# A two-layer graph kernel: three dense row chunks in place of four, and the staging order around them

## The chip, the cores and the metric

The kernel runs on one core of a Trainium2 chip. The metric is the device time of one execution in microseconds; lower is better.

## The reference

`x` is 8 x 2048 x 128 (batch, nodes, features), `adj` is a 2048 x 2048 matrix with few entries that are not zero (some nine a row). Cut to what matters:

```python
# layer 0
sj, si = inputs @ w_j, inputs @ w_i
res = si[:, :, None] + sj[:, None, :] + relation[None] * w_r + g_b
agg = einsum('bij,bjd->bid', res, inputs)
x = layernorm(x + agg @ weight + bias)
# layer 1: hops 1 and 2 over the same matrix, twice the same set of hops
x1 = einsum('bnf,nw->bwf', x0, A)
x2 = 2.0 * einsum('bnf,nw->bwf', x1, A) - x0
x = layernorm(x + relu(concat([x0, x1, x2, x1, x2]) @ Theta1 + bias))
```

So layer 0 multiplies by the rows of the matrix, layer 1 twice by its columns. All sums are in float32.

## The kernel before, in words

The nodes are cut into 16 chunks of 128. All eight batches of a chunk stand side by side: a tile of 128 x 1024 numbers, 512 KB.

**Three passes.** Layer 0 makes `y = x @ weight` for all chunks first, so that one pass over the matrix gives `agg @ weight`. Layer 1 becomes two hops with the weights folded in (`thetas`): hop 1 reads `u`, which `make_u` (lines 650 to 659) makes from the output of layer 0, and writes `y_d`; hop 2 reads `y_d` and writes the output. `make_u` transposes eight blocks of a chunk on PE, multiplies them by theta and stores 512 KB of u.

**Dense and listed chunks.** In layer 0 the first `ND` = 4 chunks of rows are multiplied in full: `full_rows` (lines 311 to 318) does 16 x 2 matmuls of 128x512 for a chunk (two records each in the profile), with the transposed rows of the matrix held in `at4`. The other twelve chunks, and all chunks of the two hops, are "listed": the matrix rows that matter for 32, 64 or 128 columns of the chunk are gathered by number. The lists are made on the chip: `mask_rows` and `mask_columns` mark the blocks that hold anything, VectorE ranks them, and `lists_end` writes row numbers into `idx`. A chunk has seven lists: four "T" lists for 32 columns each (rows of the first 14 chunks), two "H" lists for 64 columns and one for 128. For each list GpSimd (POOL) issues one indirect gather of 128 rows of 4 KB out of y, u or y_d (`get_rows`, lines 724 to 730), and `listed` (lines 732 to 755) multiplies them by the "set", the matching 128 x 384 numbers of the matrix. The diagonal block of a listed chunk is done apart: `load_own` (lines 765 to 773) has SP load the chunk's own rows and the 128 x 128 block `rd`, and `own_rows` does two matmuls.

**Sets.** A listed chunk needs two sets, one of the transposed rows for layer 0 (in `rct`) and one of the columns for the hops (in `rc`). Their sources are put side by side in DRAM: `store_rt` stores the transposed rows of a chunk into `rr_d` (1 MB), `copies` copies the matrix columns beside it (1 MB, DRAM to DRAM). `get_job` (lines 532 to 540) gathers out of `rr_d` into one of four staging buffers in `st`, with four gathers for a chunk's T lists or three for its H lists; `keep_job` (lines 542 to 563) takes them out on VectorE with four operations, two of them for each set. There are 24 such jobs, first the T jobs of all listed chunks, then the H jobs; `next_job` is a keep and a get. A get can start when the keep four jobs earlier is through. Chunks 0 to 3 have no layer-0 set, and the hop's set comes directly out of `adj`, in seven gathers a chunk (`get_direct`, lines 578 to 583), 28 in all, after `clear` has zeroed its place.

**Order.** Each engine's order is written out by hand and kept, save that the scheduler may put POOL's row gathers of the next chunk ahead of a staging gather. POOL carries the staging gathers, row gathers and directs in one queue. Row gathers go round twelve slots in `Y` (list `G`), so a gather waits until PE is through with the one twelve earlier. VectorE does, for a listed chunk of layer 0, `keep_job`, `z_add` and `layernorm` in this order. SP's queue loads the matrix, x, z (the residual x of a chunk), own rows and diagonals. The start goes: transposes and masks while the matrix arrives (to about 105 us), y and the lists, dense chunks 0 to 3 with staging beside them (lines 787 to 849), then the loop over the listed chunks:

```python
    for c in range(ND, NC):
        ...
        if kept[0] < len(jobs):
            keep_job()
        if got[0] < len(jobs):
            get_job()
        get_direct((c > 7) + (c > 9))
        accs = acc_pair()
        own_rows(0, c, accs, True)
```

Hop 1 starts with the T gathers of three chunks, for which u of chunks 0 to 13 must be stored; `make_u(15)` stands on PE behind the first chunk's T matmuls, and the H gathers wait for it.

Of the kernel before, what the change touches and what calls it, by code (L numbers as in the profile page):

```python
# [8 lines left out]
F32 = mybir.dt.float32  # L9
# [9 lines left out]
def kernel(  # L19
# [22 lines left out]
    P = 128  # L42
# [4 lines left out]
    TW = 32  # L47
    NT = N // TW
    QT = P // TW
    ND = 4  # L50
    NS = NC - ND
    LT = 14
    LR = LT // 2
    HC = NT // 2 + NC
    NI = NT + HC
    PAD = 40000
    W = 3 * P
    T_ORDER = list(range(6, NC)) + [4, 5]
    NP = LR + NC - LT
    R_ORDER = [0, 1, 4, 5, 6, 2, 7, 8, 9, 10, 3, 11, 12, 13, 14, 15]  # L60
    NX = 8
    X_ORDER = list(range(ND, NC)) + list(range(ND))
    X_SLOT = [0, 1, 3, 4, 2, 5]
    assert D == P and B == 8 and NC == 16

# [21 lines left out]

    Y = keep.tile([P, NC, B, D], F32, name="Y")
    rc = keep.tile([P, NC * W], F32, name="rc")
    rct = keep.tile([P, NS * W], F32, name="rct")  # L90
# [8 lines left out]
    def flat(t):  # L99
        return t.rearrange("p b f -> p (b f)")  # L100
# [79 lines left out]

    am = [rc[:, n * N:(n + 1) * N] for n in range(3)]
    ats = [rct[:, n * N:(n + 1) * N] for n in range(2)]
    ats += [Y[:, n:n + 2].rearrange("p c b f -> p (c b f)") for n in X_ORDER[NX::2]]

    def at_of(c):
        t = at4[:, c] if c < ND else ats[(c - ND) % len(ats)]
        return t.rearrange("p (j i) -> p j i", i=P)

    def x_at(k):
# [11 lines left out]
    todo += [("x", 8), ("s", 12), ("x", 9), ("s", 13), ("x", 10), ("x", 11), ("s", 14), ("x", 12)]  # L201
    todo += [("s", 15), ("x", 13), ("x", 14), ("x", 15)] + [("c", c) for c in T_ORDER]
    done = {"a": 0, "x": 0}

    def load_x(c, t):
# [10 lines left out]
    def pump():  # L216
        while todo:
            what, n = todo[0]
            if what == "a" and n < done["a"] + 3:
                sp.dma_start(out=am[n % 3], in_=adj[R_ORDER[n] * P:(R_ORDER[n] + 1) * P, :])  # L220
            elif what == "x" and n < done["x"] + 6:
                c = X_ORDER[n]
                xin[c] = load_x(c, ring[:, X_SLOT[n % 6]])
                if c < ND:
                    zs[c] = xin[c]
            elif what == "s" and done["a"] == NC:
                store_rt(n)
            elif what == "c" and done["a"] == NC:
                copies([n])
            else:  # L230
                return
            todo.pop(0)
# [72 lines left out]
                    tile_position=(0, 32 * j),  # L305
                )

    LAST = list(range(ND)) + list(range(8, NC)) + list(range(4, 8))
    js_first = [X_ORDER[0]] * 2 + [LAST[0]] * (ND - 2)

    def full_rows(c, accs, js):
# [211 lines left out]
    def strided(t, n, step, w):  # L523
        return t[:, 0:n * step].rearrange("p (n s) -> p n s", s=step)[:, :, 0:w]

    jobs = [("T", c) for c in T_ORDER] + [("H", c) for c in range(ND, NC)]
    got, kept = [0], [0]

    def staged(k):
# [12 lines left out]
    def keep_job():  # L542
        what, c = jobs[kept[0]]
        s = staged(kept[0])
        kept[0] += 1
        hc = has[:, columns(c, what)[0]:columns(c, what)[0] + QT]
        for k in range(2):
            to = rc[:, c * W:(c + 1) * W] if k else rct[:, (c - ND) * W:(c - ND + 1) * W]
# [168 lines left out]
    load_z(4)  # L717

    NG = 12
    G = [flat(Y[:, n]) for n in LAST[:NG]]  # L720
    g_at = [0]
    rows_of = {}

    def get_rows(i, c, what, src):
        hi = LT if what == "T" else NC
        for n, q in enumerate(columns(c, what)):
            g = G[g_at[0] % NG]
            g_at[0] += 1
            gather(g, src[0:hi * P, :], idx, q, hi * P)
            rows_of[i, c, what, n] = g  # L730

    def listed(i, c, accs, what):

        r = rc[:, c * W:(c + 1) * W] if i else rct[:, (c - ND) * W:(c - ND + 1) * W]
# [26 lines left out]
    homes = [seven[(c + 8) % 12 % 7] for c in range(12)] + [slab(k) for k in range(4)]  # L761
    u_of = [ring[:, 2]] * 12 + homes[12:]
    own = {}

    def load_own(i, src, c, t, there=False):
        if not there:
            sp.dma_start(out=flat(t), in_=src[c * P:(c + 1) * P, :])
        r = small.tile([P, P], F32, name=f"rd{i}_{c}", tag="rd", bufs=2)
        sp.dma_start(
            out=r, in_=rr_d[c - ND][c * P:(c + 1) * P, 0, :] if i == 0  # L770
            else adj[c * P:(c + 1) * P, c * P:(c + 1) * P],
        )
        own[i, c] = t, r

    def own_rows(i, c, accs, start):
        t, r = own.pop((i, c))
# [15 lines left out]
    for c0 in range(0, NC, 4):  # L792
        column_sums(c0)
    make_ub()
    load_z(ND + 1)
    rounds2([4])
    next_job()
    si_t(0)
# [12 lines left out]
    layernorm(zs[0], "0_0")  # L811

    acc2 = bank[4:6]
    full_rows(2, acc2, LAST[:5])
    next_job()
    next_job()
    make_u(0, zs[0], x1t[0], u_of[0], 0)
    layernorm(zs[1], "0_1")
    full_rows(2, acc2, LAST[5:11])
    next_job()  # L820
    make_u(1, zs[1], x1t[1], u_of[1], 0)
    next_job()
    next_job()
    next_job()
    full_rows(2, acc2, LAST[11:])
    si_t(2)
    rank9(2, acc2)
    z_add(acc2, zs[2])
    overflow()
    next_job()  # L830
    layernorm(zs[2], "0_2")

    acc3 = bank[2:4]
    full_rows(3, acc3, LAST[:8])
    next_job()
    next_job()
    get_rows(0, ND, "T", y0_d)
    get_rows(0, ND, "H", y0_d)
    own0(ND)
    own0(ND + 1)  # L840
    full_rows(3, acc3, LAST[8:])
    keep_job()
    keep_job()
    get_rows(0, ND + 1, "T", y0_d)
    si_t(3)
    rank9(3, acc3)
    si_t(ND)
    z_add(acc3, zs[3])
    layernorm(zs[3], "0_3")


    for c in range(ND, NC):
# [17 lines left out]
        listed(0, c, accs, "H")  # L870
        z_add(accs, zs[c])
        for n in [c - 2] if c < 14 else [12, 13] if c == 14 else [14]:
            make_u(n, zs[n], x1t[n], u_of[n])
        if c + 2 < NC:
            load_z(c + 2)
        rs = layernorm(zs[c], f"0_{c}")
        if c in (7, 11):
            clear((7, 11).index(c), rs[:, 0:1])


    def hop(i, src, order, there, between):
# [57 lines left out]
        for k, c in enumerate(order):  # L939
# [11 lines left out]
            if i == 1 and k in (2, 5):  # L951
                clear(2 + k // 3, homes[c][:, B - 1, 0:1])
# [6 lines left out]
    homes[4:9] = homes[9:14]  # L959
    hop(  # L960
        2, y_d, list(range(9, 14)) + list(range(ND)) + [14, 15] + list(range(4, 9)),
        list(range(ND)) + list(range(9, NC)), lambda: None,
    )


    def blocks(name, src, c, tr):
        accs = acc_pair()
        for n in range(NC):
            rows = ring[:, n % 2]
            sp.dma_start(out=flat(rows), in_=src[n * P:(n + 1) * P, :])  # L970
            r = small.tile([P, P], F32, name=f"r{name}{c}_{n}", tag="rd", bufs=2)
# [86 lines left out]
```

## Time and profile before

| | |
|---|---|
| median of 3 runs | 800.24 us (798.86 to 801.0) |
| the profiled execution | 802.74 us, of which the span of instructions is 800.9 |
| busy: PE / PEld | 725.6 us (91%) / 364.4 us (45%) |
| busy: DVE / ACT / POOL | 392.2 us (49%) / 192.8 us (24%) / 444.8 us (56%) |
| moved by DMA | 252.96 MB, mean 316 GB/s |
| POOL gathers: staging / rows of y and y_d / rows of u / direct | 84 / 196 / 112 / 28 |
| chain that ended last | PE 57%, DMA 28%, ACT 6% |

How to read it: "PE busy" is a share over stages with different limits. A row of 40 digits has the busy tenths of 20 us slices. `x64` after a PE row counts records; a float32 matmul has two. In the profile y's DRAM copy and hop 1's result both print as `y_d`, and all instructions carry line 72, where a helper issues them. What ended an idle time stands in brackets behind the row.

### The profile page before, as it was taken

How to read it: one execution, taken by the hardware profiler on the slowest of the kernel's cores; microseconds unless marked ns; L12 is line 12 of the kernel's file. 1: busy time of each engine (PE TensorE's matmuls, PEld its weight loads, DVE VectorE, ACT ScalarE, POOL GpSimd, SP SyncE). 2: the span in 40 equal slices, each digit the busy share in tenths (PEclk: the TensorE clock that was granted, in tenths of full speed). 3: DMA queues.
4: the chain of work that ended last, by engine and by line, in shares of the span. 5: the costliest groups of instructions: out<-in, count | busy, mean ns of one | idle time of the engine just before them, and what ended most of it. 6: DMA issues, size and time to landing. Idle time of an engine off the chain costs nothing.

```text
span 800.9 us, 10031 instructions
## 1 busy us (share of the span) xinstructions
PE 725.6 (91%) x3554; PEld 364.4 (45%) x3554; DVE 392.2 (49%) x572; ACT 192.8 (24%) x439; POOL 444.8 (56%) x432
## 2 busy tenths in 40 slices
PE   4999899998999989996999899889999899999992
PEld 3666566643544334443355234334444355543451
DVE  4765788785541756544451000000000577777775
ACT  3757553422210223322232000000000011111111
POOL 1000000577777775776633757777664777777740
PEclk9999999998999999999999899999999999999997
DMA  7999999999436799999989899999997899999982
GB/s 258 302 314 309 348 325 294 312 386 399 138 95 202 259 344 371 362 383 314 362 291 355 300 342 338 315 342 367 389 363 292 302 356 357 374 389 370 360 291 63
DMA packets 165299, 252.96 MB, mean 316 GB/s; under 512 B 17256, under 2 KB 118333, under 8 KB 163192
## 3 DMA queue, kind: packets, MB, share of 16 engines
q0 software_dynamic: 49280, 145.59, 50.2%
q1 hardware_dynamic: 93200, 81.01, 31.5%
q10 hardware_dynamic: 22760, 25.63, 9.0%
q8 instruction: 30, 0.49, 0.2%
q14 instruction: 29, 0.24, 0.1%
HBM read 233.77 MB, written 58.72 MB: 365 GB/s over the span
## 4 chain that ended last, share of the span: by engine, by line
PE 57%; DMA 28%; ACT 6%; issue 4%; DVE 2%; POOL 1%; ACTq 0%; POOLq 0%; SPq 0%; DVEq 0%
PE bank L72 57%; DMA Y<-u_d,idx 13%; DMA Y<-y_d,idx 9%; DMA rd<-rr_d 3%; ACT Y L72 2%; DMA ring<-in_x_dram 2%; ACT trp L72 1%; ACT rct L72 1%; ACT at L72 1%; DMA u_d<-st 1%; POOL Y L72 1%; DVE s L72 1%; DMA gb<-in_L_gnn_g_b_dram 1%; DVE st L72 1%; DVE ring L72 0%
## 5 line engine op out<-in xcount | busy, mean ns | idle before, releaser
L72 POOL DMA_INDIRECT Y<-y_d,idx x196 | 215.5, 1099 | 87.8 <-issue 36.2
L72 PE MATMUL bank<-Y,rc 128*32 128x512 f32 (+2 forms) x896 | 218.1, 608 | 20.1 <-DMA Y<-u_d,idx 17.0
L72 POOL DMA_INDIRECT st<-rr_d,idx x84 | 87.3, 1040 | 167.1 <-DVE rown L72 141.8
L72 POOL DMA_INDIRECT Y<-u_d,idx x112 | 111.3, 994 | 63.2 <-PE bank L72 22.8
L72 PEld LDWEIGHTS bank<-Y,rc 128*32 128x32 f32 (+2 forms) x896 | 59.6, 128 | 175.5 <-issue 87.7
L72 PE MATMUL bank<-Y,at 128*128 128x512 f32 x256 | 115.1, 600 | 0.0
L72 PE MATMUL bank<-Y,rct 128*32 128x512 f32 (+2 forms) x336 | 72.2, 609 | 2.8 <-DMA Y<-y_d,idx 2.7
L72 DVE TENSOR_REDUCE s<-sq 128x4 f32<-128x512 f32 x64 | 43.9, 686 | 57.1 <-ACT sq L72 57.1
L72 PEld LDWEIGHTS bank<-Y,at 128*128 128x128 f32 x256 | 47.5, 192 | 52.4 <-issue 52.2
L72 DVE COPY ring<-bank 128x512 f32<-128x512 f32 x10 | 6.9, 692 | 109.0 <-PE bank L72 109.0
L72 ACT ACTIVATE sq<-ring 128x512 f32<-128x512 f32 x44 | 27.7, 630 | 131.7 <-DVE ring L72 89.1
L72 PE MATMUL bank<-ring,rd 128*128 128x512 f32 x108 | 52.6, 611 | 6.6 <-DMA rd<-rr_d 3.9
L72 PE MATMUL bank<-ident,rc 128*128 128x128 f32 (+2 forms) x302 | 44.9, 297 | 13.2 <-DMA rc<-in_adj_dram 7.2
L72 DVE TENSOR_REDUCE st<-rc 128x64 f32<-128x2048 f32 x16 | 36.5, 2283 | 27.6 <-DMA rc<-in_adj_dram 27.6
L72 PE MATMUL bank<-th,at 128*128 128x128 f32 x384 | 48.4, 280 | 1.7 <-ACT at L72 1.7
L72 PEld LDWEIGHTS bank<-th,at 128*128 128x128 f32 x384 | 45.8, 194 | 6.8 <-ACT at L72 3.6
L72 ACT COPY ring<-bank 128x512 f32<-128x512 f32 x34 | 19.9, 586 | 116.9 <-PE bank L72 116.9
L72 PEld LDWEIGHTS bank<-ident,rc 128*128 128x128 f32 (+2 forms) x302 | 33.9, 150 | 27.1 <-issue 9.7
L72 DVE TENSOR_TENSOR ring<-bank,ring 128x512 f32<-128x512 f32 x26 | 17.2, 687 | 56.3 <-PE bank L72 44.1
L72 PEld LDWEIGHTS bank<-Y,rct 128*32 128x32 f32 (+2 forms) x336 | 19.8, 129 | 47.5 <-issue 39.1
L72 PE MATMUL bank<-wx,trp 128*128 128x130 f32 x256 | 36.5, 286 | 4.3 <-ACT trp L72 2.0
L72 PE MATMUL bank<-ident,ring 128*128 128x128 f32 x232 | 33.2, 287 | 7.1 <-DMA ring<-in_x_dram 3.0
(142 smaller groups left out, 785.5 us busy)
## 6 DMA issues: line engine op xcount, KB each, us to landing
rc<-in_adj_dram SPq DMA_DIRECT2D x16, 1024.0 KB, 11.3
ring<-in_x_dram SPq DMA_DIRECT2D x25, 512.0 KB, 9.2
rr_d<-in_adj_dram SPq DMA_DIRECT2D x12, 1024.0 KB, 11.2
rr_d<-Y SPq DMA_DIRECT2D x8, 1024.0 KB, 12.3
y_d<-Y SPq DMA_DIRECT2D x16, 512.0 KB, 10.8
u_d<-ring ACTq DMA_DIRECT2D x12, 512.0 KB
ring<-y_d SPq DMA_DIRECT2D x11, 512.0 KB
ring<-u_d SPq DMA_DIRECT2D x10, 512.0 KB, 7.1
```

The lines of the kernel that those rows point to most:

```text
L72: return lambda *a, **k: tc.keep_in_program_order(f(*a, **k))
```

## The change

`ND` goes from 4 to 3: chunk 3 becomes a listed chunk of layer 0, with its own set, staging jobs (26 in place of 24), store, copy and row gathers; its set lies in the tail of the part of `at4` that it no longer needs whole, and that part is a seventh place to hold transposed rows before they are stored. T jobs go in the order 3 to 15. The dense chunk 2 is cut differently, and chunk 3's row gathers, diagonal and own rows are issued in the middle of it (its own lists come from `idy`, a copy of `idx`). In the loop, the sets taken out in step c are those of the H lists of chunk c + 1. Directs: 21 in place of 28; 14 of them stand behind the loop in one piece, 7 in hop 1, one in a step. The diagonal `rd` of chunk c + 3 is loaded in step c, with three buffers in place of two; own rows as before two steps ahead. Layernorm of chunk 2 and make_u(2) move behind the start of chunk 3 and to step 4.

```diff
-    ND = 4
-    NS = NC - ND
+    ND = 3
...
-    T_ORDER = list(range(6, NC)) + [4, 5]
...
-    ats += [Y[:, n:n + 2].rearrange("p c b f -> p (c b f)") for n in X_ORDER[NX::2]]
+    ats += [at4[:, 3]] + [Y[:, n:n + 2].rearrange("p c b f -> p (c b f)") for n in X_ORDER[NX::2]]
+    in_turn = [n for n in R_ORDER if n >= ND]
+
+    def rct_of(c):
+        return at4[:, 3, N - W:] if c == 3 else rct[:, (c - 4) * W:(c - 3) * W]
...
-    jobs = [("T", c) for c in T_ORDER] + [("H", c) for c in range(ND, NC)]
+    jobs = [(what, c) for what in "TH" for c in range(ND, NC)]
...
+    def late_lists():
+
+        for n, w, at in ((0, QT, QT * ND), (QT, 2, NT + 2 * ND), (QT + 2, 1, NT + 2 * NC + ND)):
+            dve.tensor_copy(
+                idy[:, :, n:n + w], idx[:, at:at + 2 * w].rearrange("p (c w) -> p c w", w=w)
+            )
...
-    def load_own(i, src, c, t, there=False):
-        if not there:
-            sp.dma_start(out=flat(t), in_=src[c * P:(c + 1) * P, :])
-        r = small.tile([P, P], F32, name=f"rd{i}_{c}", tag="rd", bufs=2)
+    own, diagonal = {}, {}
+
+    def load_diagonal(i, c):
+        r = small.tile([P, P], F32, name=f"rd{i}_{c}", tag="rd", bufs=3)
...
-    acc3 = bank[2:4]
-    full_rows(3, acc3, LAST[:8])
-    next_job()
     next_job()
     get_rows(0, ND, "T", y0_d)
     get_rows(0, ND, "H", y0_d)
     own0(ND)
     own0(ND + 1)
-    full_rows(3, acc3, LAST[8:])
-    keep_job()
-    keep_job()
+    make_u(1, zs[1], x1t[1], u_of[1], 2)
+    next_job()
+    acc3 = acc_pair()
+    own_rows(0, ND, acc3, True)
+    full_rows(2, acc2, LAST[12:])
+    si_t(2)
+    rank9(2, acc2)
+    si_t(ND)
+    next_job()
     get_rows(0, ND + 1, "T", y0_d)
...
     for c in range(ND, NC):
...
-        get_direct((c > 7) + (c > 9))
-        accs = acc_pair()
-        own_rows(0, c, accs, True)
+        if c == ND:
+            accs = acc3
+        else:
+            accs = acc_pair()
+            own_rows(0, c, accs, True)
         if c + 2 < NC:
             own0(c + 2)
+        if c + 3 < NC:
+            load_diagonal(0, c + 3)
         rank9(c, accs)
...
-        if c in (7, 11):
-            clear((7, 11).index(c), rs[:, 0:1])
+        if c in (11, 13):
+            clear((11, 13).index(c), rs[:, 0:1])
+    get_direct(14)
...
-                get_direct({3: 2, 4: 2, 5: 3, 6: 1, 7: 2, 8: 2, 9: 2}.get(k, 0))
+                get_direct(2 < k < 10)
```

The order of the chunks in the hops starts at chunk 3 in place of 4 (hop 1) and at chunk 8 in place of 9 (hop 2).

More of the change, by code (lines that the diff above doesn't have):

```diff
@@ L61 @@
     NX = 8
-    X_ORDER = list(range(ND, NC)) + list(range(ND))
+    X_ORDER = list(range(4, NC)) + list(range(4))
     X_SLOT = [0, 1, 3, 4, 2, 5]
@@ L89 @@
     rc = keep.tile([P, NC * W], F32, name="rc")
-    rct = keep.tile([P, NS * W], F32, name="rct")
+    rct = keep.tile([P, 12 * W], F32, name="rct")
     at4 = keep.tile([P, 4, N], F32, name="at4")
@@ L161 @@
     has = const.tile([P, NI], F32)
+    idy = const.tile([P, 2, 7], I32)
     over = const.tile([1, 1], I32)
@@ L182 @@
     ats = [rct[:, n * N:(n + 1) * N] for n in range(2)]
-    ats += [Y[:, n:n + 2].rearrange("p c b f -> p (c b f)") for n in X_ORDER[NX::2]]
+    ats += [at4[:, 3]] + [Y[:, n:n + 2].rearrange("p c b f -> p (c b f)") for n in X_ORDER[NX::2]]
+    in_turn = [n for n in R_ORDER if n >= ND]
+    def rct_of(c):
+        return at4[:, 3, N - W:] if c == 3 else rct[:, (c - 4) * W:(c - 3) * W]
     def at_of(c):
-        t = at4[:, c] if c < ND else ats[(c - ND) % len(ats)]
+        t = at4[:, c] if c < ND else ats[in_turn.index(c) % len(ats)]
         return t.rearrange("p (j i) -> p j i", i=P)
@@ L200 @@
             todo.append(("x", x_at(k)))
-    todo += [("x", 8), ("s", 12), ("x", 9), ("s", 13), ("x", 10), ("x", 11), ("s", 14), ("x", 12)]
-    todo += [("s", 15), ("x", 13), ("x", 14), ("x", 15)] + [("c", c) for c in T_ORDER]
+    todo += [("x", 8), ("s", 13), ("x", 9), ("s", 14), ("x", 10), ("x", 11), ("s", 15), ("x", 12)]
+    todo += [("s", 12), ("x", 13), ("x", 14), ("x", 15)] + [("c", c) for c in range(ND, NC)]
     done = {"a": 0, "x": 0}
@@ L223, in pump @@
                 xin[c] = load_x(c, ring[:, X_SLOT[n % 6]])
-                if c < ND:
+                if c < 4:
                     zs[c] = xin[c]
@@ L306, in column_sums @@
                 )
-    LAST = list(range(ND)) + list(range(8, NC)) + list(range(4, 8))
+    LAST = list(range(ND)) + list(range(8, NC)) + list(range(ND, 8))
     js_first = [X_ORDER[0]] * 2 + [LAST[0]] * (ND - 2)
@@ L547, in keep_job @@
         for k in range(2):
-            to = rc[:, c * W:(c + 1) * W] if k else rct[:, (c - ND) * W:(c - ND + 1) * W]
+            to = rc[:, c * W:(c + 1) * W] if k else rct_of(c)
             of = s[:, k * P:]
@@ L719 @@
     NG = 12
-    G = [flat(Y[:, n]) for n in LAST[:NG]]
+    G = [flat(Y[:, n]) for n in LAST[7:NG - 1] + LAST[:7] + [ND]]
     g_at = [0]
@@ L728, in get_rows @@
             g_at[0] += 1
-            gather(g, src[0:hi * P, :], idx, q, hi * P)
+            first = i == 0 and c < ND + 2
+            ids, at = (idy[:, c - ND], n + QT * (what == "H")) if first else (idx, q)
+            gather(g, src[0:hi * P, :], ids, at, hi * P)
             rows_of[i, c, what, n] = g
+    def late_lists():
[3 more added lines that the diff above has]
+            )
     def listed(i, c, accs, what):
-        r = rc[:, c * W:(c + 1) * W] if i else rct[:, (c - ND) * W:(c - ND + 1) * W]
+        r = rc[:, c * W:(c + 1) * W] if i else rct_of(c)
         if what == "T":
@@ L760 @@
     seven = [ring[:, 0], ring[:, 1], ring[:, 2], spare, ring[:, 5], ring[:, 3], ring[:, 4]]
-    homes = [seven[(c + 8) % 12 % 7] for c in range(12)] + [slab(k) for k in range(4)]
+    homes = [seven[(c + 9) % 12 % 7] for c in range(12)] + [slab(k) for k in range(4)]
     u_of = [ring[:, 2]] * 12 + homes[12:]
-    own = {}
-    def load_own(i, src, c, t, there=False):
-        if not there:
-            sp.dma_start(out=flat(t), in_=src[c * P:(c + 1) * P, :])
-        r = small.tile([P, P], F32, name=f"rd{i}_{c}", tag="rd", bufs=2)
+    own, diagonal = {}, {}
+    def load_diagonal(i, c):
+        r = small.tile([P, P], F32, name=f"rd{i}_{c}", tag="rd", bufs=3)
         sp.dma_start(
@@ L772, in load_own @@
         )
-        own[i, c] = t, r
+        diagonal[i, c] = r
+    def load_own(i, src, c, t, there=False):
+        if (i, c) not in diagonal:
+            load_diagonal(i, c)
+        if not there:
+            sp.dma_start(out=flat(t), in_=src[c * P:(c + 1) * P, :])
+        own[i, c] = t, diagonal.pop((i, c))
     def own_rows(i, c, accs, start):
@@ L794 @@
     make_ub()
-    load_z(ND + 1)
+    load_z(5)
     rounds2([4])
@@ L813 @@
     acc2 = bank[4:6]
-    full_rows(2, acc2, LAST[:5])
+    full_rows(2, acc2, LAST[:7])
     next_job()
     next_job()
-    make_u(0, zs[0], x1t[0], u_of[0], 0)
+    make_u(0, zs[0], x1t[0], u_of[0], 2)
     layernorm(zs[1], "0_1")
-    full_rows(2, acc2, LAST[5:11])
-    next_job()
[L821 to L831, printed above, removed]
-    acc3 = bank[2:4]
-    full_rows(3, acc3, LAST[:8])
-    next_job()
+    late_lists()
+    full_rows(2, acc2, LAST[7:12])
     next_job()
@@ L840 @@
     own0(ND + 1)
-    full_rows(3, acc3, LAST[8:])
-    keep_job()
-    keep_job()
-    get_rows(0, ND + 1, "T", y0_d)
[L845 to L849, printed above, removed]
+    make_u(1, zs[1], x1t[1], u_of[1], 2)
[7 more added lines that the diff above has]
+    next_job()
+    get_rows(0, ND + 1, "T", y0_d)
+    next_job()
+    z_add(acc2, zs[2])
+    overflow()
     for c in range(ND, NC):
@@ L868 @@
             si_t(c + 1)
+        if c == ND:
+            layernorm(zs[2], "0_2")
         listed(0, c, accs, "T")
@@ L871 @@
         z_add(accs, zs[c])
-        for n in [c - 2] if c < 14 else [12, 13] if c == 14 else [14]:
+        for n in [] if c == ND else [c - 2] if c < 14 else [12, 13] if c == 14 else [14]:
             make_u(n, zs[n], x1t[n], u_of[n])
-        if c + 2 < NC:
+        if ND < c < NC - 2:
             load_z(c + 2)
         rs = layernorm(zs[c], f"0_{c}")
-        if c in (7, 11):
-            clear((7, 11).index(c), rs[:, 0:1])
+        if c in (11, 13):
+            clear((11, 13).index(c), rs[:, 0:1])
+    get_direct(14)
     def hop(i, src, order, there, between):
@@ L947, in hop @@
             if i == 1:
-                get_direct({3: 2, 4: 2, 5: 3, 6: 1, 7: 2, 8: 2, 9: 2}.get(k, 0))
+                get_direct(2 < k < 10)
             listed(i, c, accs[k], "H")
             end(c, accs[k])
-            if i == 1 and k in (2, 5):
-                clear(2 + k // 3, homes[c][:, B - 1, 0:1])
+            if i == 1 and k == 2:
+                clear(2, homes[c][:, B - 1, 0:1])
     hop(
@@ L958 @@
     assert kept[0] == len(jobs) and not direct
-    homes[4:9] = homes[9:14]
+    homes[3:8] = homes[8:13]
     hop(
-        2, y_d, list(range(9, 14)) + list(range(ND)) + [14, 15] + list(range(4, 9)),
-        list(range(ND)) + list(range(9, NC)), lambda: None,
+        2, y_d, list(range(8, 14)) + list(range(ND)) + [14, 15] + list(range(ND, 8)),
+        list(range(ND)) + list(range(8, NC)), lambda: None,
     )
@@ L970, in blocks @@
             sp.dma_start(out=flat(rows), in_=src[n * P:(n + 1) * P, :])
-            r = small.tile([P, P], F32, name=f"r{name}{c}_{n}", tag="rd", bufs=2)
+            r = small.tile([P, P], F32, name=f"r{name}{c}_{n}", tag="rd", bufs=3)
             i, j = (c, n) if tr else (n, c)
```

## The prediction

> **What bounds the kernel now.** I read the 40-slice rows first, then the busy time by stage, then the timelines of POOL, PE and DVE where one stage hands over to the next.
>
> ```profile
> PE   4999899998999989996999899889999899999992
> POOL 1000000577777775776633757777664777777740
> DMA  7999999999436799999989899999997899999982
> ```
>
> A 7 in POOL's row is a full queue: a gather shows 1.00 us and the next starts 0.30 us later, so 77% is all that can show. DMA has one hole, slices 11 to 13 (200 to 260 us), and POOL is full just there.
>
> ```profile
> 190.00:230.00 40.00, 36.49 (x117) 18.99 (x115) 18.55 (x44) 9.25 (x16) 31.11 (x30) 0.94 0.60 197
> 230.00:259.00 29.00, 28.65 (x73) 12.57 (x71) 10.87 (x30) 1.82 (x4) 22.66 (x21) 1.00 0.51 150
> 259.00:299.00 40.00, 36.68 (x169) 14.96 (x166) 23.76 (x41) 9.88 (x21) 31.24 (x29) 0.96 0.88 301
> 299.00:359.00 60.00, 58.57 (x312) 27.43 (x311) 35.00 (x53) 20.64 (x42) 42.68 (x42) 1.00 1.01 371
> 359.00:417.00 58.00, 49.94 (x261) 23.87 (x261) 27.95 (x38) 17.27 (x34) 30.74 (x31) 0.97 0.91 325
> 460.00:568.00 108.00, 96.66 (x433) 40.17 (x432) 7.03 (x11) 5.06 (x10) 77.51 (x78) 1.00 0.94 346
> 568.00:609.00 41.00, 39.91 (x194) 17.55 (x193) 2.77 (x4) 2.45 (x5) 27.73 (x28) 1.00 1.00 373
> ```
>
> Columns: stretch, then busy time of PE, PEld, DVE, ACT, POOL, then granted clock, DMA share, GB/s. From 190 to 259 PE is full with the dense rows of chunks 2 and 3, and POOL is full with staging (30 gathers in 40 us); neither waits for the other. From 259 to 299 chunks 4 to 6 run off POOL's lists and PE has holes. From 299 to 359 PE is full again (11.8 us a chunk), from 359 to 417 it has 8 us of holes. In hop 1, to 568, POOL is full (78 gathers in 108 us), and only after that DMA.
>
> ```profile
> 237.60 1.00 POOL L72 DMA_INDIRECT Y<-y_d,idx  x1 [0.30 <-PE bank L72]
> ...
> 272.00 1.81 POOL L72 DMA_INDIRECT Y<-y_d,idx  x1 [0.30 <-issue]
> ...
> 401.16 1.00 POOL L72 DMA_INDIRECT rc<-in_adj_dram,idr  x1 [0.30 <-DMA u_d<-ring]
> 402.47 1.00 POOL L72 DMA_INDIRECT rc<-in_adj_dram,idr  x1 [0.30 <-issue]
> 413.90 1.19 POOL L72 DMA_INDIRECT Y<-u_d,idx  x1 [10.42 <-PE bank L72]
> ```
>
> POOL has issued without a pause since 145.06. The first row gather comes as number 70, chunk 5's last (272.00) as number 95. Before hop 1 POOL stands idle 10.42 us.
>
> ```profile
> 230.19 27.73 PE L72 MATMUL bank<-Y,at 128*128 128x512 f32 x64
> 274.49 6.88 PE L72 MATMUL bank<-Y,rct 128*32 128x512 f32 x28
> 293.13 5.49 PE L72 MATMUL bank<-Y,rct 128*64 128x512 f32 x10 [2.73 <-DMA Y<-y_d,idx]
> 351.95 5.71 PE L72 MATMUL bank<-Y,rct 128*32 128x512 f32 x28
> 379.42 3.61 PE L72 MATMUL bank<-ring,rd 128*128 128x512 f32 x4 [3.87 <-DMA rd<-rr_d]
> 411.34 5.71 PE L72 MATMUL bank<-Y,rct 128*32 128x512 f32 x28
> ```
>
> The first row is dense chunk 3; then the list matmuls of chunk 5 (end 281.4), 6 (the wait), 11 (end 357.7), 13's diagonal (the wait), 15 (end 417.1).
>
> **What is removed.** Chunk 3's 64 dense records, 27.7 us. As a listed chunk it costs PE 1.88 (diagonal) + 5.71 (lists): 20.1 us of PE work less, and PE can begin listed chunks some 28 us sooner. Whether that reaches the end depends on POOL.
>
> **Staging and row gathers, POOL.** The new listed chunk adds 7 staging and 7 row gathers. In the built order of the changed kernel chunk 3's last row gather is number 65, chunk 4's 84, chunk 5's 94. Number 65 was at 230.2 in this trace and number 94 at 270.7; so PE, ready at about 230, gets chunk 3 at once, then waits some 20 us for chunk 4, and chunk 5 again ends at 281, where it ends now. PE's saving is gone by then. What is late next is POOL: seven more sets of three staging gathers are still ahead, one in front of each chunk's rows up to 11; before, staging ended with chunk 6.
>
> **A new wait.** From chunk 6 on, the three staging gathers in front of chunk c+1's lists need a staging buffer that VectorE empties at the start of chunk c, behind the layernorm of chunk c-1. Queued behind them on POOL are the rows for which PE waits.
>
> ```profile
> 281.41 0.69 DVE L72 TENSOR_TENSOR trp<-bank,trp 128x512 f32<-128x512 f32 x1 [0.17 <-PE bank L72]
> ...
> 290.64 0.37 DVE L72 TENSOR_SCALAR rc<-st,has 128x128 f32<-128x128 f32 x1
> ```
>
> So from the end of chunk c-1 (281.4) to the buffer's release (291.0) 9.6 us; then 3 staging gathers 3.9, five row gathers until the last starts 6.5, 0.5 for gathers stretched by VectorE (number 95 took 1.81), 7.4 until it has landed (272.00, used at 279.38), and 1.9 for its four records: 29.8 us from the end of chunk c-1 to that of c+1, 14.9 a chunk. Nothing in the trace of before shows this wait. From below it is bounded by POOL's own ten gathers at 1.30 (13.0; the stretched pace of 230 to 257 us, 1.40, gives 14.0), from above by landings of 9 us, as between 305 and 400, with PE at half clock after its waits: 15.8. I take 14.9, the sum of the nearest rows.
>
> Chunks 6 to 11: 6 x 14.9 = 89.4 against 357.7 - 281.4 = 76.3 now, **+13.1**. Chunks 12 to 15 then run without staging: 4 x 11.8 + 3.7 for the second make_u of chunk 14, and 0.5 for a late load, 51.4 against 417.1 - 357.7 = 59.4, **-8.0**: the holes before chunks 12 and 13 came after five chunks at 371 GB/s, and at 14.9 us a chunk no backlog builds up. The diagonal's earlier load is inside this (3.87 at most): SP issues the own rows just ahead of it as before, so alone it would uncover the next wait. If the backlog returns, the 8.0 do too.
>
> **The rule of the clock.** The Trainium skill (TensorE: Matmul & The Clock Gate, Part 1: The HAM clock gate) says that the array falls to half clock after an idle window of about 3.4 us. That speaks against a change that makes PE wait. The row at 293.13 is harsher: after 2.73 us idle, ten records took 5.49 where 5.71 - 2.93 = 2.8 is usual for the same ten (287.47 holds the first 18, 2.93). By the rule the new waits (3.1 us a chunk, in two or three pieces) cost nothing; by the row up to 2.7 in each round of two chunks, 8.1 over six. A wait of 2.69 at 363.5 cost nothing (1.96 for 1.88). I take nothing in the sum, and the row in a rival.
>
> **Direct gathers.** Fourteen stood between the rows of layer 0, where POOL had time; they now stand in one piece before hop 1's first rows, 14 x 1.30 = 18.2 us. POOL is through with chunk 15 at 401.2, so those rows start at 419.4 in place of 413.9: +5.5. PE waits for them (to 425.7), and u's last chunk and the second lists hang on it. They took 7.7 from issue to landing because loads and stores of the same moment were in the way; later these have drained, 5.5: **+3.4** (1.5 to 5.5). In hop 1 seven of 14 remain: POOL gets 9.1 us back while it is the bound. Chunks with directs take 11.8 us there, those after 568 take 10.2, at 373 GB/s: DMA gives back part, I take **-6.5** (-2 to -9.1).
>
> **Staging of R, SP and VectorE before 190.** One more 1 MB store and one more 1 MB copy (44.4 us for 12, 3.7 each) in a full DMA. The last adj row chunk landed at 97.4 and PE used it at 100.2, the next x is as near: **+1.5** (0 to 3). The copy moves SP's stores of y0 from 186 to 192; first read at 218, free. One more column mask of 2.3 us lies in 4.2 us of VectorE's waits before 107. The list copies (about 0.2 each) stand in VectorE's idle time before 230. Layernorm of chunk 2 moves behind chunk 3's start, where PE waits for gathers.
>
> **Sum:** 1.5 + 13.1 - 8.0 + 3.4 - 6.5 = +3.5, on the profiled 802.7: 806.2. The median of the runs is 2.5 below that execution, so 803.7. Hop 2 stays PE's (11.6 us a chunk, no holes).
>
> **Rivals.**
> - *POOL's own pace sets the chunks, not the round through VectorE* (0.24). Between 237 and 262 us gathers landed as early as 4.2 us after their issue, 5.2 after its start. With that and no stretched gather the round is 29.8 - 2.2 - 0.5 = 27.1, 13.6 a chunk, which POOL's ten gathers need about as well: 6 x 1.3 = 7.8 less, 795.9, faster. It decides below 13.9. For it: DMA has room there. Against: own rows, z and u share it from chunk 6 on.
> - *It cancels* (0.20): between 13.9 and 14.7 a chunk, about 800.
> - *PE cold and late landings* (0.13): 15.8 a chunk, +5.4, and the store's 3 us: 811.
> - *The dense rows' 20 us come through* (0.03): 784. POOL's count speaks against it: chunk 11 needs gather number 154, at 1.30 not before 345.
>
> **Numbers.** Forecast 0.40; slower 0.53, same 0.20, faster 0.27. A measurement tells about 0.3%, 2.4 us. The range goes from the first rival to the third, 793 to 812.
>
> **What would show it.** Right: PE idle 15 to 20 us between chunks 3 and 4; chunk 5's lists ending near 281; staging gathers before 350 us that wait for VectorE; 14 to 15.5 us a chunk to chunk 11; no long wait for rd; 14 directs in a row on POOL and PE waiting behind them; hop 1 chunks of 10.5 us. Wrong: a chunk under 13.9 us from 6 to 11, or PE waits for adj before 190 of more than 3 us.

## The result, and the profile after

| | before | after |
|---|---|---|
| median of 6 runs | 800.62 us (798.68 to 805.03) | 818.24 us (817.15 to 819.88) |
| ratio, 95% interval | | 1.0229 (1.0202 to 1.0255) |
| profiled execution / span | 802.74 / 800.9 | 818.9 / 817.1 |

Slower, as the forecast had the direction, but by 17.6 us where it had 3.5, and outside its range. One set of four runs further down was made while the kernel before took 856.3 us, so these four are compared with each other alone.

The 40 slices of the kernel after, rows as before:

```profile
PE   4998899999995888989997999999999899999992
...
POOL 1000000577777666577657476776664677776750
PEclk9999999999996999989998999999999999999997
DMA  7999999999656898989996899999999799999982
```

The hole that was DMA's alone (slices 11 to 13) is now PE's too: slice 13 has PE at 5 and the clock at 6. POOL's row is no longer a string of sevens: between 260 and 340 us it stands at six and five.

Busy time by stage, kernel after; columns: stretch, PE, PEld, DVE, ACT, POOL, granted clock, DMA share, GB/s:

```profile
190.00:230.00 40.00, 37.48 (x123) 19.03 (x123) 19.37 (x49) 9.15 (x16) 31.26 (x29) 0.96 0.79 274
230.00:259.00 29.00, 23.15 (x65) 5.39 (x61) 15.22 (x27) 3.79 (x9) 22.60 (x22) 0.76 0.61 198
259.00:299.00 40.00, 29.75 (x123) 12.30 (x124) 15.20 (x26) 7.90 (x16) 28.23 (x28) 0.91 0.82 271
299.00:359.00 60.00, 53.93 (x232) 22.47 (x230) 30.93 (x52) 15.81 (x32) 37.97 (x37) 0.93 0.87 305
359.00:417.00 58.00, 54.05 (x267) 23.66 (x268) 31.28 (x54) 15.81 (x32) 39.35 (x38) 0.96 1.00 365
```

Before, 299 to 359 held 312 PE records in 58.57 us at a clock of 1.00 (0.188 us each). Now it holds 232 in 53.93 us at 0.93 (0.232 each): fewer records in nearly the same busy time, so part of "busy" is a slower clock.

Where the time went, marked by the first transposes behind a chunk's lists on PE (that is the chunk's end) and, for hop 1, by POOL's first H gather:

| stretch | before | after | difference | the sum had |
|---|---|---|---|---|
| start to end of chunk 5 | 281.21 | 284.60 | +3.4 | +1.5 |
| chunks 6 to 11 | 76.28 | 96.24 | +20.0 | +13.1 |
| chunks 12 to 15 | 59.39 | 52.14 | -7.3 | -8.0 |
| end of chunk 15 to first H gather of hop 1 | 22.34 | 28.93 | +6.6 | +3.4 |
| from there to hop 2's first transposes | 188.62 | 182.64 | -6.0 | -6.5 |
| the rest | 173.1 | 172.6 | -0.5 | 0 |

PE's timeline of the kernel after, from chunk 3's end to chunk 8's (start, length, engine, what it does; in brackets the idle time ahead and what ended it):

```profile
248.16 1.91 PE L70 MATMUL bank<-Y,rct 128*32 128x512 f32 x2 [2.54 <-DMA Y<-y_d,idy]
...
263.00 6.84 PE L70 MATMUL bank<-Y,rct 128*64 128x512 f32 x12 [5.09 <-DMA Y<-y_d,idy]
...
304.60 1.04 PE L70 MATMUL bank<-ident,ring 128*128 128x128 f32 x8
...
310.87 5.79 PE L70 MATMUL bank<-Y,rct 128*32 128x512 f32 x28
...
324.37 1.05 PE L70 MATMUL bank<-Y,rct 128*32 128x512 f32 x2 [0.57 <-DMA Y<-y_d,idx]
328.01 1.04 PE L70 MATMUL bank<-Y,rct 128*32 128x512 f32 x2 [2.60 <-DMA Y<-y_d,idx]
329.65 7.23 PE L70 MATMUL bank<-Y,rct 128*32 128x512 f32 x22 [0.59 <-DMA Y<-y_d,idx]
336.72 1.04 PE L70 MATMUL bank<-ident,ring 128*128 128x128 f32 x8
```

Chunk 3 is done early (at 242.5), and PE then waits for chunk 4's gathers. It stands idle 8.8 us in four pieces there, where 15 to 20 us were forecast, and between them it works at a low clock (0.76 from 230 to 259 us). Later the chunks go in pairs: chunk 7 ends 11.9 us after chunk 6 (no wait), chunk 8 20.2 after chunk 7. In chunk 8 PE waits 3.8 us in three pieces and the 22 records behind take 7.23 us. POOL over the same stretch:

```profile
314.38 1.00 POOL L70 DMA_INDIRECT st<-rr_d,idx  x1 [5.11 <-DVE rc L70]
...
318.30 1.00 POOL L70 DMA_INDIRECT Y<-y_d,idx  x1 [0.31 <-issue]
...
325.17 1.11 POOL L70 DMA_INDIRECT Y<-y_d,idx  x1 [0.30 <-issue]
```

and VectorE, which ends that wait of 5.11 us:

```profile
304.81 0.69 DVE L70 TENSOR_TENSOR ring<-bank,ring 128x512 f32<-128x512 f32 x1 [0.17 <-PE bank L70]
...
312.29 1.22 DVE L70 TENSOR_TENSOR ring<-ring,rs 128x1024 f32<-128x1024 f32 x1
313.43 0.28 DVE L70 TENSOR_TENSOR rct<-st,has 128x128 f32<-128x128 f32 x1
...
314.03 0.28 DVE L70 TENSOR_SCALAR rc<-st,has 128x128 f32<-128x128 f32 x1
```

This is the forecast wait: end of chunk 6 (304.60), layernorm, then the set taken out, release at 314.3. Up to chunk 8's last row gather (325.17) the round takes 9.8 + 10.8 us, as the sum had it. From there to chunk 8's end it takes 11.6 where the sum had 9.3.

What the clock does behind the short waits of chunks 6, 8 and 10 (columns as above, the clock third from the right; the third row is the first two records of chunk 10, behind a wait of 0.75 us):

```profile
298.63:304.60 5.97, 5.97 (x12) 2.02 (x13) 0.65 (x1) 0.00 (x0) 4.62 (x5) 0.71 0.93 322
329.65:336.72 7.07, 7.07 (x23) 1.86 (x23) 0.66 (x1) 0.00 (x0) 5.50 (x6) 0.78 0.82 298
356.58:358.43 1.85, 1.85 (x2) 0.14 (x2) 1.75 (x5) 0.00 (x0) 1.41 (x2) 0.53 0.99 399
360.26:368.18 7.92, 7.92 (x24) 2.08 (x25) 0.66 (x1) 0.00 (x0) 6.09 (x7) 0.79 0.88 291
```

Length times the missing share of the clock gives 1.7, 1.6 and 1.7 us in the first, second and last row. That is an estimate of what the clock took at these three chunks, 5.0 us together, if no late landing stands right behind it.

### The profile page after: what moved, and what is told of

Same layout as the page of the kernel before. It is cut to its first block, busy times and chain, and to the rows that moved or that the text cites. A ratio compares the mean times of both kernels' runs of the same rounds, so it can differ in the third digit from the quotient of the medians.

```text
span 817.1 us, 10033 instructions
## 1 busy us (share of the span) xinstructions
PE 731.5 (90%) x3522; PEld 359.5 (44%) x3522; DVE 396.6 (49%) x581; ACT 192.5 (24%) x439; POOL 452.2 (55%) x439
## 4 chain that ended last, share of the span: by engine, by line
DMA 43%; PE 38%; issue 7%; ACT 5%; DVE 3%; POOL 3%; ACTq 0%; POOLq 0%; SPq 0%; DVEq 0%
PE bank L70 38%; DMA Y<-y_d,idx 16%; DMA Y<-u_d,idx 15%; DMA st<-rr_d,idx 5%; DMA ring<-in_x_dram 3%; ACT Y L70 2%; POOL Y L70 1%; POOL st L70 1%; DMA rc<-in_adj_dram,idr 1%; DVE s L70 1%; ACT rct L70 1%; DMA y_d<-st 1%; ACT trp L70 1%; ACT at L70 1%; DMA Y<-y_d,idy 1%
## 5 line engine op out<-in xcount | busy, mean ns | idle before, releaser
L70 POOL DMA_INDIRECT Y<-y_d,idx x189 | 207.4, 1097 | 83.0 <-issue 34.1
L70 PE MATMUL bank<-Y,rc 128*32 128x512 f32 (+2 forms) x896 | 222.5, 612 | 16.1 <-DMA Y<-u_d,idx 13.3
L70 POOL DMA_INDIRECT st<-rr_d,idx x91 | 95.0, 1044 | 185.4 <-DVE rown L70 144.8
L70 PE MATMUL bank<-Y,rct 128*32 128x512 f32 (+2 forms) x336 | 94.3, 674 | 22.6 <-DMA Y<-y_d,idx 13.8
L70 PE MATMUL bank<-Y,at 128*128 128x512 f32 (+2 forms) x220 | 96.5, 619 | 0.9 <-DMA Y<-y_d,idy 0.9
L70 PEld LDWEIGHTS bank<-Y,rct 128*32 128x32 f32 (+2 forms) x336 | 23.2, 136 | 86.0 <-issue 44.7
L70 PEld LDWEIGHTS bank<-Y,at 128*128 128x128 f32 (+2 forms) x220 | 37.9, 187 | 44.9 <-issue 39.8
L70 DVE TENSOR_TENSOR ring<-bank,ring 128x512 f32<-128x512 f32 x26 | 17.6, 690 | 62.9 <-PE bank L70 62.9
## 6 DMA issues: line engine op xcount, KB each, us to landing
y_d<-Y SPq DMA_DIRECT2D x16, 512.0 KB, 10.7
```

Of the source, the lines that this page charges most:

```text
L70: return lambda *a, **k: tc.keep_in_program_order(f(*a, **k))
```

## Experiments on the round through VectorE

Theory: the staging gathers wait for VectorE's set, the rows stand behind them on POOL, and two chunks take what this round takes. The round is longer than forecast because PE's clock falls in its waits. Rivals: landings in a full DMA set the pace, or late landings stand right behind the clock, so that a faster PE would only wait for them.

**The set taken out a chunk sooner** (in the loop):

```diff
-        if kept[0] < len(jobs):
+        if c == ND:
             keep_job()
...
         listed(0, c, accs, "H")
+        if kept[0] < len(jobs):
+            keep_job()
         z_add(accs, zs[c])
```

> The changed kernel with one thing moved: VectorE takes a staged set out one chunk sooner, behind the layernorm of the chunk before the last instead of behind that of the last, so that POOL's staging gathers of chunks 6 to 11 find their buffer free. Theory (a round through VectorE sets the pairs of chunks): the waits of POOL for VectorE go, the pairs of 20 and 12 us go, and POOL's ten gathers set the pace, 13 to 14 us a chunk instead of 16.0, so 12 to 18 us less: about 804 us. Rival (the landings of gathers in a shared DMA set it): chunks stay at 15 us or more and the time above 812 us.

808.47 us, ratio to before 1.0094 (1.0066 to 1.0121), 9.8 below the changed kernel. POOL and stages of this kernel:

```profile
300.35 1.01 POOL L70 DMA_INDIRECT st<-rr_d,idx  x1 [0.30 <-DVE s L70]
...
314.20 1.80 POOL L70 DMA_INDIRECT st<-rr_d,idx  x1 [0.30 <-DVE s L70]
```

```profile
299.00:359.00 60.00, 55.78 (x272) 25.37 (x269) 34.30 (x57) 18.81 (x38) 45.34 (x43) 1.00 0.98 356
366.00:391.00 25.00, 23.49 (x123) 10.86 (x122) 14.99 (x27) 7.91 (x16) 15.24 (x15) 1.00 1.01 375
391.00:411.00 20.00, 16.49 (x62) 6.37 (x61) 7.57 (x11) 4.06 (x8) 7.25 (x8) 0.74 0.88 315
```

No staging gather waits any more (0.30 is POOL's own gap), chunks 7 to 11 end 13.7 us apart, and chunks 6 to 11 take 79.8 us, 16.5 less (83.2 and 82.7 in two later kernels with the same edit). With these waits gone, DMA at 356 GB/s does not hold the chunks at 15 us; the rival falls. But half comes back: chunks 12 to 15 now take 60.2 us. DMA has stood at 375 GB/s for two chunks, and PE then waits 3.3 us at chunk 14's own rows; the issues of own rows in SP's queue take 8.1 and 11.8 us just there (last row: clock 0.74). This execution took 812.0 us, 3.5 more than the median, so part of the hole may be its own.

**PE kept busy.** First, four matmuls whose result is not used, one ahead of each T list of the first half of chunks 6, 8 and 10:

```diff
                 for t in range(QT):
+                    if i == 0 and h == 0 and c in (6, 8, 10):
+                        pe.matmul(bank[5], ident, th[:, 0:4, :]..., start=True, stop=True)
```

> The changed kernel with four added matmuls of 128x512 whose result is not used, one ahead of each of the first four T matmuls of chunks 6, 8 and 10 in layer 0, that is inside PE's waits there (3.8 us of waits at chunk 8, four matmuls take some 3.5 us). Theory (PE's clock falls in these waits and the 22 records behind them then take 7.2 us instead of 4.9): they come back to about 5, 2.3 us less at each of three chunks, so about 811 us. Rival (these records are slow for another reason, such as H rows that land late): no gain, 818 us, or up to 3 us more where the added matmuls delay the first lists.

811.51 us, as the theory had it, and yet no proof: in its trace chunks 6 to 11 took 95.6 us, 0.7 less. The last 22 records did take 5.68 us, but the added matmuls between the lists cost as much as the waits had, and the scheduler had moved POOL's order (below). Its chunk 5 ended 3.2 us sooner, ahead of any edit; chunks 12 to 15 were 1.4 shorter, and the step to the first H gather 2.3. So three matmuls were put together ahead of the lists:

```diff
         if what == "T":
+            for n in range(3 if i == 0 and c in (6, 8, 10) else 0):
+                pe.matmul(bank[5], ident, th[:, 0:4, :]..., start=True, stop=True)
             for h in range(2):
```

> The changed kernel itself once more, beside the three below. Expected 818, between 816 and 820, with two chunks of steps 6 to 11 taking 32 us together. The four profiles that so far share its early part start POOL's staging between 145.8 and 148.1 us, so its chunk 5 ends anywhere from 281 to 285.

> The changed kernel with three added matmuls of 128x512 (result not used, 2.9 us) in one block ahead of the first T matmuls of chunks 6, 8 and 10 of layer 0. The run with four added matmuls between the lists came out 6.7 us lower, but its trace shows only 0.7 us of that in chunks 6 to 11, where its added matmuls took more than the waits had, so it does not decide. This one leaves the lists together. Theory (the last term of the round, 11.7 us in place of 9.3, is PE's clock after its waits): the last 22 to 24 records take 5.7 us in place of 7.2 to 8.1, and chunks 6 to 11 get 4 to 6 us shorter, 812 to 814. Rival (late landings stand behind the clock, 8 to 11 us from issue in a full DMA): less than 2 us, 816 to 819.

In that set, with the kernel before at 856.3, the changed kernel took 895.24 and this one 887.18, 8.1 less: the sign, but no size for the other traces. Again, with the kernel before at 800.99:

> The changed kernel with three added matmuls (result not used) in one block ahead of the first T matmuls of chunks 6, 8 and 10, once more, because in the last set the kernel before itself took 856 us. As before: if the last term of the round is PE's clock after its waits, chunks 6 to 11 take 90 to 92 us in place of 96 and the time is 812 to 814; if late landings stand behind the clock, less than 2 us are gained, 816 to 819. In the last set this kernel was 8 us below the changed one.

813.52 us, ratio 1.0162 (1.0134 to 1.0190), 4.7 below the changed kernel. PE of this kernel in chunk 8:

```profile
321.88 2.74 PE L70 MATMUL bank<-th,ident 128*128 128x512 f32 x6
324.55 2.98 PE L70 MATMUL bank<-Y,rct 128*32 128x512 f32 x18
329.13 3.84 PE L70 MATMUL bank<-Y,rct 128*64 128x512 f32 x10 [1.60 <-DMA Y<-y_d,idx]
332.81 1.04 PE L70 MATMUL bank<-ident,ring 128*128 128x128 f32 x8
```

2.74 us of added work, and the lists behind it run at full clock: ten records in 3.84, chunk 8's end at 332.81. Chunks 6 to 11 take 91.6 us, 4.6 less, at a mean clock of 1.00 in place of 0.93 (the row below, columns as before); two chunks take 30.5 us on the mean, where the forecast had 29.8. In four profiles that leave these steps as they are in the changed kernel, chunks 6 to 11 take 96.2 to 98.2 us.

```profile
283.31:374.92 91.61, 82.43 (x385) 36.54 (x384) 45.84 (x79) 23.72 (x48) 64.06 (x62) 1.00 0.94 330
```

This does not price the clock by itself, because the scheduler has moved POOL's order too. Between the groups of staging gathers from chunk 5 on the changed kernel has seven row gathers each time; this kernel has 7, 8, 7, 8 and 7 (the one with four matmuls 7, 9, 7, 8 and 7). So chunks 8 and 9 have one more of their seven gathers ahead of the staging, chunks 10 and 11 two more:

```profile
311.21 1.00 POOL L70 DMA_INDIRECT st<-rr_d,idx  x1 [2.72 <-DVE rc L70]
...
320.49 0.99 POOL L70 DMA_INDIRECT Y<-y_d,idx  x1 [0.30 <-issue]
```

From the buffer's release to the last row gather this kernel takes 9.3 us at chunk 8 and 8.1 at chunk 10, where the changed kernel took 10.8 and 10.7. From there to the chunk's end, where the clock would show, it takes 12.3 and 10.5 in place of 11.6 and 11.0; the last gather of chunk 8 landed 10.1 us after its issue. So the clock is back, but the 3.8 us won between the ends of chunks 6 and 10 stand in POOL's part of the round. The rival of late landings is not ruled out, and the clock's share of the missing term stays the estimate above.

## Experiments on the block of direct gathers

**The directs back in the loop:**

```diff
             get_job()
+        get_direct((c > 7) + (c > 9))
...
-        if c in (11, 13):
-            clear((11, 13).index(c), rs[:, 0:1])
-    get_direct(14)
+        if c in (7, 11):
+            clear((7, 11).index(c), rs[:, 0:1])
```

> The changed kernel with one thing undone: the fourteen direct gathers of chunks 0 and 1 stand in the loop again (one in steps 8 and 9, two in steps 10 to 15), and the two sets are cleared in steps 7 and 11. My theory now: as one block before hop 1 they cost 9.3 us there (first row gather of hop 1 at 6.14 us after chunk 15's end instead of 3.15 us ahead of it); in the loop, steps 12 to 15 have room for eight of them, but the six in steps 8 to 11 stand in POOL's round, 1.30 us each, so up to 7.8 us come back. Expected about 813 us, between 809 and 817, with hop 1's first T matmuls ending 10 to 12 us after chunk 15. Rival, that the late start of hop 1 has another cause (u of the last chunks stored late, loads in the way): no change, 818 us or more.

822.42 us, slower than the changed kernel; the expectation missed. The step from chunk 15 to the first H gather did shrink, to 21.2 us (7.7 less). But chunks 6 to 11 took 104.3 us, 8.0 more, which is six directs at 1.30, and chunks 12 to 15 4.5 more. I had given the eight of steps 12 to 15 room that is not there.

**The block in the kernel before:**

```diff
-        get_direct((c > 7) + (c > 9))
...
+    get_direct(14)
```

> The kernel before with only one part of the change: the fourteen direct gathers of layer 0's loop stand in one block behind the loop. Theory from the changed kernel's trace: the block of 18 to 22 us starts when POOL is through with chunk 15's rows and delays hop 1's first rows from 3 us before chunk 15's end to 6 us after it, and hop 1's first lists run at a lower clock: 6 to 9 us more, 807 to 810 us. The prediction's value for this part was 3.4 us, 804 us. If steps 8 to 15 gain from a POOL without directs, up to 3 us less than either.

802.26 us, ratio 1.0018 (0.9999 to 1.0036): no price that can be told from zero, so both numbers missed. There POOL is far ahead of PE, the first u gather still starts 3.9 us ahead of chunk 15's end, and the first H gather comes 21.8 us behind it. The block costs only where POOL is late.

**The changed kernel without the block:**

```diff
-    get_direct(14)
+    del direct[:14]
```

> The changed kernel without the fourteen direct gathers of chunks 0 and 1 (it leaves these out: the sets of chunks 0 and 1 stay zero in the hops). It prices the block. Theory (the block makes hop 1's first H gather come 28.9 us after chunk 15's end in place of 22.3): 6 to 8 us less, 810 to 812. The prediction's value for the block was 3.4 us net: 815. Rival (another part of the change holds up hop 1): no change.

In the set of 856.3: 883.13 against 895.24. Again:

> The changed kernel without the fourteen direct gathers of chunks 0 and 1 (it leaves these out: the sets of chunks 0 and 1 stay zero in the hops), once more for the same reason. If the block's price is what the place of the first H gather shows (6.6 us), 810 to 812; if the prediction's 3.4 us, 815; in the last set this kernel was 12 us below the changed one, which would make 806.

813.02 us, ratio 1.0161 (1.0131 to 1.0191): by the medians the block's price is 5.2 us, between the two values, with runs from 809.2 to 814.9. The gathers are left out whole, so the price holds their transfers too. The first u gather of this kernel:

```profile
428.87 0.99 POOL L70 DMA_INDIRECT Y<-u_d,idx  x1 [15.21 <-DMA ring<-u_d]
```

POOL stands idle 15.21 us and still starts only 0.8 us ahead of chunk 15's end: what it waits for comes then. So a block up to some 15 us long would be hidden here; the block took 22.0 (417.26 to 439.29), of which four gathers of the kernel after say why it is more than 14 x 1.30:

```profile
426.32 0.99 POOL L70 DMA_INDIRECT rc<-in_adj_dram,idr  x1 [1.04 <-DMA Y<-y_d,idx]
429.38 1.80 POOL L70 DMA_INDIRECT rc<-in_adj_dram,idr  x1 [2.07 <-DVE rs L70]
...
437.99 1.00 POOL L70 DMA_INDIRECT rc<-in_adj_dram,idr  x1 [0.30 <-issue]
439.29 1.00 POOL L70 DMA_INDIRECT Y<-u_d,idx  x1 [0.30 <-DMA rc<-in_adj_dram,idr]
```

**The places cleared two steps sooner** (`(9, 11)` in place of `(11, 13)`), against the 2.07 us for layernorm 13:

> The changed kernel with the two places cleared two steps sooner, in steps 9 and 11. The block's eighth gather then does not wait for layernorm 13 (2.07 us before it, and 0.8 us longer by itself). Theory: the block takes 19 to 20 us in place of 22.0 and the time is 2 us less, 816. Rival (the block's length is set by the gathers eight places ahead, which land late): no change, 818.

892.44 us in the set of 856.3, 2.8 below the changed kernel's 895.24 with runs that spread from 884 to 904: undecided.

**The block spread**, with the set taken out sooner: chunk 0's directs in steps 12 to 15, chunk 1's behind hop 1's first T gathers (the two places are cleared in steps 9 and 14):

```diff
+        if c > 11:
+            get_direct(2 - c // 15)
...
-    get_direct(14)
...
         begun = len(accs)
+        if i == 1:
+            get_direct(7)
```

> The changed kernel with VectorE's keep a chunk sooner (as in the run with 808.5 us) and the block of fourteen directs spread: chunk 0's seven in steps 12 to 15 of the loop, where POOL has three staging gathers fewer to do and waits for PE's slots, chunk 1's seven between hop 1's first T gathers and its first H gather, where POOL waits 9.8 us for u of chunk 15. Theory (directs cost nothing where POOL is idle and their issue time where it is not): the first H gather of hop 1 comes 22 us after chunk 15's end instead of 28.7, so 6 to 7 us less: 802, between 799 and 805. Rival (steps 12 to 15 have no room either, as in the run with directs in steps 8 to 15): chunks 12 to 15 get up to 7 us longer and the time stays at 808.

802.90 us, the expected number, though not by the expected way: the first H gather comes 26.5 us after chunk 15's end, only 2.2 sooner, because the seven directs behind the T gathers reach past the moment u is ready. Chunks 12 to 15 took 53.8 us in place of 60.2, which I had not expected and which no run explains.

## Experiments on the smaller steps

**Chunk 3's store behind the last x** (the `store_rt` of the loop from `ND + 1` on, `("s", 3)` at the end of the load list):

> The changed kernel with one thing moved: the 1 MB store of chunk 3's transposed rows goes behind the last load of x, so that it no longer stands among the loads of the matrix and of x. Theory (this store is what makes adj and x land late, 3.0 us at 110 us of the trace): 2 to 3 us less, 815.5, and POOL's first staging gather back at 145 to 146 us. Rival (the lateness comes from VectorE's added column mask or from the changed order of T jobs): no change, 818.

815.65 us, ratio 1.0209 (1.0167 to 1.0251): by the time alone it can't be told from the changed kernel. In the traces POOL's first staging gather comes at 144.5, and at 145.4 in the last run below, which has the same edit. Eight profiles that share the changed kernel's early part start it at 145.7 to 148.1, mean 146.8, six of before at 144.2 to 145.1, mean 144.7. So the store is what makes the start late. This step costs 2.1 us by the means, and the changed kernel's own profile happened to be 1.3 later.

**The diagonal**, a chunk sooner in the kernel before, and as before in the changed one (`load_diagonal` of `c + 3` taken out of the loop):

> The kernel before with only the diagonal blocks loaded a chunk sooner (three buffers in place of two). The prediction said that this alone would uncover the next wait, because SP issues the own rows just ahead of the diagonal as before and DMA stands at 371 GB/s: less than 1.5 us of the 3.87 us wait come back, 799 to 801. Rival (the diagonal's place in the queue is the whole wait): 3 to 4 us less, 796.5.

> The changed kernel with the diagonal blocks loaded when the kernel before loads them (the three buffers stay). Theory (chunks 12 to 15 lost their holes because 16 us a chunk before them leave no backlog in DMA, not because the diagonal comes sooner): no change, 817 to 819. Rival (the sooner diagonal took the 3.87 us wait away): 3 to 8 us more, 821 or above.

800.47 us, ratio 1.0013 (0.9995 to 1.0031), and 820.41 us, ratio 1.0250 (1.0213 to 1.0287), whose interval overlaps the changed kernel's. In the first the wait of 3.87 us for `rd` is gone, but one of 3.74 stands ahead of chunk 12 and chunk 12 takes 19.0 us. The next wait was uncovered; the part is worth nothing that can be told.

**Hop 1's directs in POOL's idle time, kernel before.** Seven ahead of the first T gathers (`clear(2)` in step 13, `get_direct(7)` behind the loop), then also the other seven between T and H gathers:

> The kernel before with seven of hop 1's fourteen direct gathers (chunk 2's) moved to where POOL stands idle 10.42 us ahead of hop 1's first row gathers; 7 x 1.30 = 9.1 us fit there. Theory (POOL is the bound of hop 1, each direct there costs its 1.30 us): up to 9.1 us less, as the changed kernel's hop 1 with seven fewer directs took 172.9 in place of 182.0 us; expected 792.5, between 791 and 795. Rival (DMA takes over as the bound of hop 1's chunks): less than 3 us, 798 or more.

> The kernel before with all fourteen of hop 1's direct gathers moved into POOL's two idle stretches: seven ahead of the first T gathers of hop 1 (10.42 us idle), seven between the last of these T gathers and the first H gather (9.88 us idle, waiting for u of chunk 15). Theory (POOL bound in hop 1 until DMA is): chunks with directs take 11.8 us, those without 10.2, so seven chunks x 1.6 = 11 us less; expected 789, between 785 and 792. Rival (the directs get in the way of u's last store and of the first T rows): the second seven bring nothing, 793 or more.

797.59 us, ratio 0.9968 (0.9955 to 0.9982), and 795.63, ratio 0.9964 (0.9946 to 0.9981). Stages of hop 1, with seven moved and with fourteen:

```profile
460.00:568.00 108.00, 100.92 (x466) 43.40 (x468) 7.32 (x11) 5.86 (x10) 74.58 (x76) 1.00 0.97 364
```

```profile
460.00:568.00 108.00, 101.75 (x477) 43.01 (x475) 6.92 (x10) 5.26 (x9) 68.33 (x70) 1.00 0.98 371
```

Before, DMA stood at 346 GB/s here and POOL at 78 gathers. With seven fewer DMA is at 364, and the next seven take 6 us of work from POOL for 7 GB/s: the bound has passed to DMA. In the profiles hop 1 is 5.8 us shorter with seven moved, as in the changed kernel; by the medians only 2.4 of it is left, and I cannot say where the rest goes. Both are still the fastest kernels here. Fourteen moved together with the sooner diagonal:

> The kernel before with hop 1's fourteen directs in POOL's two idle stretches (795.6 us by itself) and the diagonals loaded a chunk sooner. If the sooner diagonal is worth its wait alone, 792; if it uncovers the next wait, 795 to 796.

797.34 us, ratio 0.9961 (0.9945 to 0.9976): nothing more. And all that helped, in the changed kernel (set sooner, late store, no direct left in hop 1's chunks):

> The changed kernel with what the runs so far point to: keep a chunk sooner, chunk 3's store behind the last x, no direct gather in a place where POOL is the bound (chunk 0's in steps 12 to 15, chunk 1's ahead of hop 1's first rows where POOL was seen idle 13.65 us, chunk 2's ahead of the first H rows). From 802.9 for the run without the last two: 2.6 less for the store, 3 to 6 less for hop 1 without directs; expected 796, between 793 and 799. If the time from chunk 15's end to the first H rows grows again, 800 or more.

799.92 us, ratio 1.0008 (0.9994 to 1.0021): these edits bring the changed kernel back to the time of before, not below it. The expected 796 missed: the first H gather came 25.8 us after chunk 15's end, again held by the seven directs in front of it.

## Why the prediction was wrong

The trace (818.9) lies 12.7 us above the sum's 806.2: 6.9 of it in chunks 6 to 11, 3.2 in the step to hop 1, 1.9 in the early part, the rest in pieces under 1 us.

- *"I take nothing in the sum, and the row in a rival"* is the step that failed. The clock's price was read off a row and then left out, because one wait of 2.69 us had cost nothing. In the changed kernel the clock falls at chunks 6, 8 and 10 behind waits of which none is over 2.6 us: at chunk 8, 22 records take 7.23 us in place of 5.68. By the clock's rows it took some 5.0 of the 6.9 us missing in chunks 6 to 11. This is an estimate; the run with three matmuls brings the clock back and is 4.6 us shorter there, but its gathers stand in another order too, so no run prices the clock alone. The row at 293.13 was also read too dear: its ten records take 3.84 us at full clock when they stand apart from the first 18, as in that run, and not 2.8, so the clock had cost 1.7 there and not 2.7. A rule of one idle window of 3.4 us (the Trainium skill, TensorE: Matmul & The Clock Gate, Part 1: The HAM clock gate), taken for a single wait, would have made it nothing; the measurement decides.
- *"7.4 until it has landed"*: the rest of the round's error, as far as is known. Seven row gathers around chunk 8's landed 8.1 us after issue in the middle, as slow as they landed in the kernel before at 300 to 340 us (8.6). That is 0.7 more in a round, some 2 us over three.
- *The mechanism* was right: the wait for VectorE's set, its place, its 9.6 us and its pairs of chunks are in the trace, and removing it alone gives the first rival's pace (13.7 measured, 13.6 written). The third rival, "PE cold and late landings", is the nearest to the case that came; its 15.8 us a chunk met 16.0, but its 811 took over the sum's other terms. One sign failed: PE's 15 to 20 us of idle time between chunks 3 and 4 were 8.8.
- *"14 x 1.30 = 18.2"*, net 3.4: the block took 22.0, for the clear behind layernorm 13 and waits for earlier gathers, and its last direct kept the first u rows to 6.3 us behind chunk 15's end. Its price is 5.2 by the run without it, within 1.5 to 5.5, and 6.6 in the trace.
- *Early part, +1.5*: 2.1 by the profiles' means, inside its 0 to 3. *Hop 1, -6.5*: -6.0. *The diagonal, nothing*: so.
- *Chunks 12 to 15, -8.0*: -7.3. That the missing backlog is the reason is not shown: with the wait taken away the time came back in one trace (60.2 us), but not in the two others with that edit (53.8 and 53.2), which have seven directs in these steps.

## What to carry to other kernels

A wait that is added to a round is paid twice: by its length, and by what the matmuls behind it lose in clock; price both from the row that shows it and do not average it away with a row that does not. POOL's issue time is free only up to the moment for which POOL would have waited anyway: fourteen gathers in one block cost nothing in the kernel before and 5 us in the changed one, and in the changed one's loop chunks 6 to 15 grew by 12.5 us. A total that comes out as expected proves little: look in the trace for where the time came from, and whether the edit has moved another engine's order.

## What the runs showed of the hardware

PE's clock also falls behind short waits. Behind 0.57, 2.60 and 0.59 us, with about 1.0 us of work between each, 22 records took 1.5 us longer than at full clock. At chunk 10 the clock stood at 0.53 behind a first wait of 0.75 us. No threshold comes out of these runs: a wait of 2.69 us cost nothing in the kernel before, and one of 2.21 us at chunk 7 of the run with four added matmuls left four records at 3.65 us in place of 1.96. With 2.74 us of unused matmuls ahead of the lists the clock stayed at 1.00.

The same early code varied by 2.4 us in when its list was ready, from one execution to another, which is more than some of the steps above are worth.
